# Cross attention: turning the probabilities with transfers of 16-bit halves in place of TensorE transposes

## The chip, the cores and the metric

The kernel runs on one core of a Trainium2 chip. The metric is the device time of one execution in microseconds (us), as the median of several runs. The core has a matrix engine (TensorE, "PE" in the profile; its weight loads are "PEld"), a vector engine (VectorE, "DVE"), a scalar engine (ScalarE, "ACT"), GpSimd ("POOL") and the engine that issues nearly all transfers here (SyncE, "SP"). Each engine runs its own queue of instructions in order and waits on semaphores for the others. SBUF is the on-chip working memory with 128 partitions; PSUM is the small memory that TensorE writes to.

## What is computed

One layer of a perceiver: cross attention of 64 latents per batch to 512 context rows (and to the latents themselves), then self attention over the latents, then a feed-forward part whose weights and activations are quantised to 4 bits. There are 16 batches, 512 channels, and 8 heads of 64 channels in the cross attention, which is all that the change touches:

```python
    def _L0_xattn_ref(x, latents, mask, g_x, b_x, g_l, b_l, w_q, w_kv, w_out, g_o, b_o):
        ...
        xn = _ln(x, g_x, b_x)
        ln = _ln(latents, g_l, b_l)
        q = ln @ w_q
        kv_in = jnp.concatenate([xn, ln], axis=1)
        k, v = jnp.split(kv_in @ w_kv, 2, axis=-1)
        ...
        sim = jnp.einsum('bhid,bhjd->bhij', q, k)
        ...
        attn = jax.nn.softmax(sim, axis=-1)
        out = jnp.einsum('bhij,bhjd->bhid', attn, v)
        out = out.transpose(0, 2, 1, 3).reshape(B, Lq, H * DH)
        return _ln(out @ w_out, g_o, b_o)
```

## The kernel before

**Stages.** First the latents are normalised and projected, and the weights of the keys and values are prepared (`latents`). Then follows the loop over the 16 batches (`cross_attention`), with the quantisation of the feed-forward weights spread over it in small steps (`quant.tick`). Then come the self attention and the feed-forward part. The change lies in the loop over the batches alone.

**One batch.** `keys(b, m)` makes a quarter of the keys, m = 0 to 3: 12 matmuls into one PSUM bank `pk`, which VectorE scales into `k`. `values(b, t)` does the same for a quarter of the values: 12 matmuls into `pv`, which ScalarE scales into `v` (L954). `scores(b, a)` makes the scores of half of the heads (a = 0, 1) into two PSUM tiles `sim`, `softmax(b, a)` has VectorE take the minimum and ScalarE the exponential; the probabilities `pr` come out with the latents on the partitions: 128 partitions (two heads of 64 latents) by 2 (r, two pairs of heads) by 576 columns. The sum of the rows is divided out later. To be the stationary operand of the weighing, the probabilities of the 512 context rows must have the context rows on the partitions. So they are turned.

**The turn.** `turn(b)` turns the probabilities in 32 transposes on TensorE (L1004, 64 x 128 each) into two PSUM tiles `prt`, which come from the same pool of two as the scores (`cm.two`). ScalarE copies these out in four copies (L1013) into `prT`. `turn_latents(b)` turns the last part, the probabilities of the 64 latents, in two transposes (L1023) into `prlt`, which ScalarE copies into `prl`. `finish(b)` then multiplies: `weigh_latents` with `prl` and the latents' values `vl`, then `weigh(b, a, r)` four times with `prT` and `v` into `av`, and `collect` divides by the sums.

**The order.** The loop is written out by hand as a pipeline: in the turn of the loop for batch b, the probabilities of batch b - 1 are turned after the first keys of b, and weighed after the first scores of b. In short, on TensorE:

```python
        keys(b, 0)
        if b:
            turn(b - 1)
            turn_latents(b - 1)
        if done is not None:
            out_turn(done)
        keys(b, 1); keys(b, 2); keys(b, 3)
        scores(b, 0)
        finish(b - 1)
        scores(b, 1)
        values(b, 0); values(b, 1)
        if done is not None:
            out_product(done)
        values(b, 2); values(b, 3)
```

`done` is set in odd batches from 3 on: the output projection of two earlier batches, whose input is turned in `out_turn` (`ot`, 4 transposes) and multiplied in `out_product` (`po`, 12 matmuls). So an odd batch has more work on TensorE than an even one.

**Buffers.** `pk`, `pv`, `ot`, `po` and half of `av` share the three PSUM banks of the pool `mm`: each needs a bank that has been read out. In SBUF, `pr` has two buffers, `prT` four, `v` four; the tag `two_h` (two buffers) holds `prl`, and `two_l` (two buffers) holds `vl`.

**Transfers.** Everything goes through SP's queue, in program order: per batch four loads of the turned context (`raw`, from `fetch`, 256 KB each), one of the context itself (`nat`, 1 MB, from `load`), eight small ones for the latents' keys (`k<-k_d`), four of row factors (`rs_d`), one each of `row`, `mu` and `mask`, two of `vl`, and the loads and stores of the quantised weights (`qw`, `g_d`, `u_d`, `d_d`).

Of the kernel before, what the change touches and what calls it, by code (L numbers as in the profile page):

```python
# [9 lines left out]
F32 = mybir.dt.float32  # L10
F32R = mybir.dt.float32r
U32 = mybir.dt.uint32
U8 = mybir.dt.uint8
AF = mybir.ActivationFunctionType
ALU = mybir.AluOpType
AX = mybir.AxisListType
# [3 lines left out]
P = 128  # L20
D = 512
KC = D // P
B = 16
S = 64
N = 512
NJ = N // P
# [24 lines left out]
class Common:  # L51
# [112 lines left out]
    def shifted(self, dst, src, mv):  # L164

        self.nc.scalar.activation(dst, src, AF.Identity, bias=mv[:, 2:3], scale=mv[:, 1:2])

# [692 lines left out]
def cross_attention(tc, cm, sc, i, cw, cx, w1, w2, att, quant):  # L860

    nc = tc.nc
# [24 lines left out]
    state = {}  # L887
    half = (N + S) // 2

    def begin(b):  # L890
        if b >= B:
            return
        p, e = divmod(b, 2)
        g, n = divmod(b, GB)
        mine = slice(n * S, (n + 1) * S)
        mu = w1.tile([P, N], U8, tag="mu", name=f"mu_{b}")
        nc.sync.dma_start(mu, i["mask"][b : b + 1, :].to_broadcast([P, N]))
        with nc.allow_non_contiguous_dma(reason="the latents of a batch"):
            nc.sync.dma_start(queries[e], sc.q[g][:, :, mine])
        state[b] = dict(mu=mu, k=[], v=[], tot=cm.small.tile([P, KC], F32, tag="tot", name=f"tot_{b}"))  # L900

    def latents_values(b):
        if b >= B:
            return
        p, e = divmod(b, 2)
        vl = state[b]["vl"] = w2.tile([P, KC, S], F32, tag="two_l", bufs=2, name=f"vl_{b}")
        src = sc.v[p][e * S : (e + 1) * S].rearrange("p (n two d) -> p n two d", two=2, d=S)
        for h in range(2):
            nc.sync.dma_start(vl[h * S : (h + 1) * S], src[:, :, h, :])
# [22 lines left out]
    def keys(b, m):  # L932

        k = ends.pop((b, m))
        hi, lo = cx.done[b]
        cols = slice(m * P, (m + 1) * P)
        ps = cm.mm(f"pk_{b}_{m}")
        cm.product(
            ps, lambda c: (w_k[0][:, c, cols], w_k[1][:, c, cols], hi[:, c, :], lo[:, c, :]), range(KC)
        )  # L940
        nc.vector.tensor_tensor(k[:, S : S + N], ps, cx.row[b], ALU.mult)  # L941
        state[b]["k"].append(k)

    def values(b, t):
        hi, lo = cx.done[b]
        cols = slice(t * P, (t + 1) * P)
        ps = cm.mm(f"pv_{b}_{t}")
        cm.product(
            ps,
            lambda k: (hi[:, k, cols], lo[:, k, cols], w_v[0][:, k, :], w_v[1][:, k, :]),  # L950
            range(KC),
        )
        v = w1.tile([P, D], F32, tag="v", bufs=4, name=f"v_{b}_{t}")
        nc.scalar.mul(v, ps, cx.rs[b][:, t : t + 1])  # L954
        state[b]["v"].append(v)
# [18 lines left out]

    def softmax(b, a):
        st = state[b]
        st["pr", a] = w1.tile([P, 2, N + S], F32, tag="pr", bufs=2, name=f"pr_{b}_{a}")

        def two(t):
            return t.rearrange("p (h n) -> p h n", h=2)  # L980

        for r, ps in enumerate(st.pop(("sim", a))):
            mask = masks[b % 2][:, columns_of(r)[0]]
            pr = st["pr", a][:, r, :]
            least = cm.small.tile([P, 1], F32, tag="least", name=f"least_{b}_{a}_{r}")
            nc.vector.tensor_tensor_reduce(  # L986
                two(pr), ps[:, :, :half], two(mask), -1.0, BIG, ALU.add, ALU.min, least
            )
            t = 2 * a + r
            nc.scalar.activation(  # L990
                pr, pr, AF.Exp, bias=least, scale=-1.0, accum_out=st["tot"][:, t : t + 1]
            )

    def turn(b):

        pts = [cm.two(f"prt_{b}_{a}") for a in range(2)]
        for a, pt in enumerate(pts):
            for r in range(2):
                first = columns_of(r)[1].start
                for j in range(NJ):  # L1000
                    at = (r * NJ + j) * S
                    for c in range(2):
                        rows = slice(c * S, (c + 1) * S)
                        nc.tensor.transpose(  # L1004
                            pt[:, c, at : at + S],
                            state[b]["pr", a][rows, r, first + j * P : first + (j + 1) * P],
                            cm.ident[rows, rows],
                        )
        for a, pt in enumerate(pts):
            for r in range(2):  # L1010
                prT = w1.tile([P, NJ, P], F32, tag="prT", bufs=4, name=f"prT_{b}_{a}_{r}")
                src = pt[:, :, r * NJ * S : (r + 1) * NJ * S].rearrange("p c (j q) -> p c j q", q=S)
                nc.scalar.copy(prT.rearrange("p j (c q) -> p c j q", q=S), src)  # L1013
                state[b]["prT", a, r] = prT

    def turn_latents(b):
        st = state[b]
        prl = w2.tile([P, 2, P], F32, tag="two_h", bufs=2, name=f"prl_{b}")
        pt = cm.ps_av.tile([P, D], F32, tag="av", name=f"prlt_{b}")[:, : 2 * P]
        pt = pt.rearrange("p (n q) -> p n q", q=P)  # L1020
        for a in range(2):
            pr = st.pop(("pr", a)).rearrange("p r t -> p (r t)")
            nc.tensor.transpose(pt[:, a, :], pr[:, N : N + P], cm.ident)  # L1023
        nc.scalar.copy(prl, pt)
        st["prl"] = prl

    def weigh_latents(b):

# [123 lines left out]
    for b in range(B):  # L1152

        def tick():
            if b:
                quant.tick()

        done = (b - 3) // 2 if b >= 3 and b % 2 else None
        last = b == B - 1
        keys(b, 0)  # L1160
        if last:
            att.load("Wq")
            att.load("Wk")
        cx.high(b + 1, 0)
        if b >= 4 and b % 2 == 0:
            out_moments((b - 4) // 2)
        if b > 1:
            tick()
        if b:
            turn(b - 1)  # L1170
            turn_latents(b - 1)
        if done is not None:
            out_turn(done)
        keys(b, 1)
        cx.low(b + 1, 0)
        cx.high(b + 1, 1)
        if b > 1:
            tick()
        keys(b, 2)
        if done is not None:  # L1180
            out_low(done)
        cx.fetch(b + 2, 0)
        if b == 0:
            for k in range(KC):
                load_o(k)
        cx.flat(b + 1)
        cx.low(b + 1, 1)
        cx.high(b + 1, 2)
        tick()
        if last:  # L1190
            att.split("Wq", 0, 1)
        if b == 0:
            scores(b, 0)
            softmax(b, 0)
        keys(b, 3)
        cx.fetch(b + 2, 1)
        if b:
            scores(b, 0)
            softmax(b, 0)
        cx.low(b + 1, 2)  # L1200
        cx.high(b + 1, 3)
# [3 lines that stand above are left out]
            softmax(b, 1)  # L1205
            around(b + 1, 2, 3)
            around(b + 2, 0, 1)
        tick()
        values(b, 0)
        cx.every(b + 1)  # L1210
        cx.low(b + 1, 3)
        cx.stats(b + 2, 0)
        tick()
        if last:
            att.split("Wq", 2, 3)
            att.load("Wv")
        if b == 0:
            scores(b, 1)
            softmax(b, 1)
            around(b + 1, 2, 3)  # L1220
            around(b + 2, 0, 1)
        values(b, 1)
        begin(b + 1)
        latents_values(b + 1)
        cx.fetch(b + 2, 2)
        cx.stats(b + 2, 1)
        tick()
        if last:
            att.norm(0)
            att.split("Wk", 0, 1)  # L1230
        tick()
        if done is not None:
            out_product(done)
        tick()
        values(b, 2)
        cx.fetch(b + 2, 3)
        cx.stats(b + 2, 2)
        tick()
        if done is not None:
            out_norm(done)  # L1240
            out_add(done)
        if b == 0:
            weight_o(0)
            weight_o(1)
        if b == 2:
            att.sa.load()
        if b == 5:
            att.sa.work()
        if last:
            att.split("Wk", 2, 3)  # L1250
            att.load("Wo")
            att.turn(0)
        values(b, 3)
        cx.stats(b + 2, 3)
        cx.spread(b + 2)
        mask(b + 1)
        if b == 0:
            weight_o(2)
            weight_o(3)
        quant.tick()  # L1260
        cx.load(b + 3)
    turn(B - 1)
    turn_latents(B - 1)
# [691 lines left out]
```

## Time and profile before

| what | value |
|---|---|
| median of 3 runs | 880.91 us (880.81 to 881.11) |
| the profiled execution | 881.33 us, span 879.5 us |
| TensorE clock granted | 1.0 throughout |
| `prt` on TensorE (L1004), 512 transposes | 19.3 us busy |
| `prlt` on TensorE (L1023), 32 transposes | 7.0 us busy |
| `prT` on ScalarE (L1013), 64 copies | 32.6 us busy, 594 ns each |
| `pr`, the exponential on ScalarE (L990), 64 | 49.1 us busy, 769 ns each |
| `v` on ScalarE (L954), 64 | 43.2 us busy, 684 ns each |
| transfers issued from SP | 109.48 MB, 38.2% of 16 engines' span |

The span is the time from the first to the last instruction in the trace; the execution's own time is a little longer. A line of the groups names the line of code, the engine, the operation, the tile written and the tiles read, the shape, how many there were, their busy time and the mean of one, and then the idle time of the engine ahead of them with what ended it. L121 is the line of a helper that issues nearly all matmuls, so matmuls are told apart by tile. In a timeline each line is a merged run of like instructions with its start and length in us. For SP it shows the issuing of transfers, not their flight.

### The profile page before, as it was taken

The numbers are of one execution on the slowest core, as the hardware profiler recorded it, in microseconds if no ns is written. First come the engines' busy times: TensorE is split into PE (matmuls) and PEld (weight loads), VectorE is DVE, ScalarE is ACT, GpSimd is POOL, SyncE is SP. The second block draws the span as 40 slices with busy tenths as digits, with TensorE's granted clock in tenths as the row PEclk, the third lists the DMA queues.
The fourth block names the chain that finished last, engine by engine and source line by source line (L and its number), as shares of the span: only waits on it lengthen the run. The fifth ranks groups of instructions, "written<-read, shape, count | busy, mean of one in ns | idle before, by whom it ended". The sixth has DMA issues, their size and how long they took to land.

```text
span 879.5 us, 17521 instructions
## 1 busy us (share of the span) xinstructions
PE 871.7 (99%) x6743; PEld 719.2 (82%) x6743; DVE 687.2 (78%) x1457; ACT 398.8 (45%) x787; POOL 296.2 (34%) x341
## 2 busy tenths in 40 slices
PE   8999999999999999999999999999999999999998
PEld 8988787878787888778878888888888888888887
DVE  7734457789788887787888867688998897888876
ACT  5654454544544535354445455554556233332221
POOL 2334234235353352353433622545543120111100
PEclk9999999999999999999999999999999999999999
DMA  8464554644655455435644362240008330000000
GB/s 277 167 233 169 167 163 142 201 143 141 192 164 160 138 174 168 136 111 178 183 134 149 121 198 64 82 192 1 1 3 320 136 144 13 13 13 13 13 12 25
DMA packets 80379, 111.12 MB, mean 126 GB/s; under 512 B 33176, under 2 KB 39080, under 8 KB 79016
## 3 DMA queue, kind: packets, MB, share of 16 engines
q1 hardware_dynamic: 80136, 109.48, 38.2%
q8 instruction: 53, 0.87, 0.4%
q0 software_dynamic: 160, 0.52, 0.2%
q14 instruction: 30, 0.25, 0.1%
HBM read 84.26 MB, written 25.72 MB: 125 GB/s over the span
## 4 chain that ended last, share of the span: by engine, by line
PE 93%; DVE 3%; DMA 2%; ACT 1%; POOL 1%; issue 1%; SPq 0%; ACTq 0%; DVEq 0%; POOLq 0%
PE pv L121 20%; PE pk L121 19%; PE gu L121 13%; PE dn L121 6%; PE sim L967 4%; PE av L1055 4%; PE Wv L121 3%; PE wo L121 3%; PE po L121 2%; PE Wq L121 2%; PE Wk L121 2%; PE prt L1004 2%; PE lq L121 2%; PE lk L121 2%; PE lv L121 1%; PE ht L171 1%
## 5 line engine op out<-in xcount | busy, mean ns | idle before, releaser
L121 PE MATMUL pv<-xvh,x 128*128 128x512 f32 x512 | 133.0, 394 | 0.0
L121 PE MATMUL pk<-x,xkh 128*128 128x512 f32 x512 | 128.2, 392 | 0.0
L121 PEld LDWEIGHTS pv<-xvh,x 128*128 128x128 f32 x512 | 94.8, 188 | 26.2 <-issue 7.0
L121 PEld LDWEIGHTS pk<-x,xkh 128*128 128x128 f32 x512 | 94.9, 188 | 19.5 <-issue 0.4
L990 ACT ACTIVATE pr<-pr,least 128x576 f32<-128x576 f32 x64 | 49.1, 769 | 59.7 <-DVE least L986 59.7
L941 DVE TENSOR_TENSOR k<-pk,row 128x512 f32<-128x512 f32 x64 | 43.2, 675 | 39.2 <-PE pk L121 39.0
L368 POOL TENSOR_TENSOR x<-raw,x 128x512 fp32r<-128x512 f32 x32 | 41.6, 1301 | 85.8 <-ACT x L362 80.5
L121 PE MATMUL pv<-xvl,x 128*128 128x512 f32 x256 | 68.7, 390 | 0.0
L121 PE MATMUL pk<-x,xkl 128*128 128x512 f32 x256 | 68.5, 389 | 0.0
L954 ACT ACTIVATE v<-pv,rs 128x512 f32<-128x512 f32 x64 | 43.2, 684 | 54.8 <-PE pv L121 54.3
L121 PE MATMUL gu<-uT,fx 128*128 128x512 f32 (+1 forms) x288 | 67.0, 377 | 0.2 <-DMA uT<-u_d 0.2
L121 PE MATMUL gu<-gT,fx 128*128 128x512 f32 (+1 forms) x288 | 65.8, 376 | 0.0
L121 PEld LDWEIGHTS gu<-gT,fx 128*128 128x128 f32 x288 | 52.2, 188 | 7.6 <-ACT fx L129 0.2
L121 PEld LDWEIGHTS gu<-uT,fx 128*128 128x128 f32 x288 | 51.8, 188 | 7.7 <-DMA uT<-u_d 0.5
L121 PEld LDWEIGHTS pv<-xvl,x 128*128 128x128 f32 x256 | 48.0, 188 | 10.3
L121 PEld LDWEIGHTS pk<-x,xkl 128*128 128x128 f32 x256 | 48.1, 188 | 10.2
L986 DVE CUSTOM_DVE_ANT_0 pr<-sim,mask 128x576 f32<-128x576 f32 x64 | 45.8, 753 | 5.3 <-PE sim L967 4.3
L205 ACT ACTIVATE qe_h<-qe_h,mmagic 128x512 f32<-128x512 f32 (+1 forms) x24 | 16.5, 687 | 66.7 <-DVE qe_h L202 64.6
L321 DVE BATCH_NORM_STATS2 cst<-nat 128x6 f32<-128x512 f32 x64 | 42.8, 669 | 3.7 <-DMA nat<-in_ctx_dram 3.7
L121 PE MATMUL dn<-dT,hh 128*128 128x512 f32 x170 | 42.9, 392 | 0.0
L967 PE MATMUL sim<-k,mask 64*64 64x288 f32 x512 | 40.4, 415 | 0.3 <-DMA mask<-q_d 0.3
L362 ACT CAST x<-raw 128x512 fp32r<-128x512 f32 x64 | 39.1, 631 | 0.0
(347 smaller groups left out, 1867.1 us busy)
## 6 DMA issues: line engine op xcount, KB each, us to landing
nat<-in_ctx_dram SPq DMA_DIRECT2D x16, 1024.0 KB
raw<-in_ctxT_dram SPq DMA_DIRECT2D x64, 256.0 KB
d_d<-qhl_d SPq DMA_DIRECT2D x11, 512.0 KB
row<-rs_d SPq DMA_DIRECT2D x16, 256.0 KB
g_d<-qhl_g SPq DMA_DIRECT2D x8, 512.0 KB
u_d<-qhl_u SPq DMA_DIRECT2D x8, 512.0 KB
gT<-g_d SPq DMA_DIRECT2D x4, 1024.0 KB
uT<-u_d SPq DMA_DIRECT2D x4, 1024.0 KB
```

The costliest lines, as they stand in the source:

```text
L121: self.nc.tensor.matmul(ps, lhsT=p[i], rhs=p[j], start=start and n == 0, stop=stop and n == last)
L205: nc.scalar.activation(e, e, AF.Relu, bias=self.mmagic, scale=MAGIC)
L321: nc.vector.bn_stats(st, self.nat[b][:, j, :])
L362: self.cm.nc.scalar.copy(self.done[b][0][:, c, :], self.raw[:, c, :])
L368: by.tensor_tensor(lo, self.raw[:, c, :], f32(hi), ALU.subtract)
L941: nc.vector.tensor_tensor(k[:, S : S + N], ps, cx.row[b], ALU.mult)
L954: nc.scalar.mul(v, ps, cx.rs[b][:, t : t + 1])
L967: nc.tensor.matmul(pss[r][c * S : (c + 1) * S, h, :half], lhsT=queries[b % 2][rows, m, :], rhs=st["k"][m][rows, at : at + half], start=Tru ...
L986: nc.vector.tensor_tensor_reduce(two(pr), ps[:, :, :half], two(mask), -1.0, BIG, ALU.add, ALU.min, least)
L990: nc.scalar.activation(pr, pr, AF.Exp, bias=least, scale=-1.0, accum_out=st["tot"][:, t : t + 1])
L1004: nc.tensor.transpose(pt[:, c, at : at + S], state[b]["pr", a][rows, r, first + j * P : first + (j + 1) * P], cm.ident[rows, rows],)
L1055: nc.tensor.matmul(st["av"][r][rows, a, :], lhsT=prT[:, j, rows], rhs=st["v"][j][:, at : at + S], start=False, stop=j == NJ - 1, skip_grou ...
```

## The change

The turn of the context's probabilities leaves TensorE in batches 0 to 14; the last batch keeps `turn`. In its place stand three steps.

`halves(b, a)`: ScalarE takes the 32-bit probabilities of the context columns apart into their lower and upper 16 bits, in two copies of 128 x 1024 16-bit elements (`half`, which takes over the two buffers of `two_h`). `send(b, a)`: SP issues two transposing transfers from SBUF to SBUF, one for each half, 256 KB each, into `far`, which takes a buffer of `pr` (so that pool's buffers now go round as `pr`, `pr`, `far`, `far`; it grows by 64 elements a row to keep the needed columns together). `join(b, a)`: ScalarE writes both halves back into 32-bit `prT`, in two copies (r = 0, 1), each of 1024 16-bit elements, interleaved.

`turn_latents(b)` moves from the next batch's first keys to the place between the second and third values of its own batch, and `prl` becomes the second part of the tile that holds `vl`.

In the order of the program, `halves(b, 0)` stands after the first values, `halves(b, 1)` and then `send(b, 0)` after the third values (the `send` behind the batch's last `raw` load), `send(b, 1)` after the fourth, ahead of the `nat` load; `join(b - 1, 0)` stands after the second keys of the next batch, `join(b - 1, 1)` after the third.

```diff
@@ latents_values
-        vl = state[b]["vl"] = w2.tile([P, KC, S], F32, tag="two_l", bufs=2, name=f"vl_{b}")
+        both = w2.tile([P, 2, KC * S], F32, tag="two_l", bufs=2, name=f"lat_{b}")
+        vl = state[b]["vl"] = both[:, 0].rearrange("p (n d) -> p n d", d=S)
+        state[b]["prl"] = both[:, 1].rearrange("p (n q) -> p n q", q=P)
@@ softmax
-        st["pr", a] = w1.tile([P, 2, N + S], F32, tag="pr", bufs=2, name=f"pr_{b}_{a}")
+        wide = w1.tile([P, 2 * (N + 2 * S)], F32, tag="pr", bufs=2, name=f"pr_{b}_{a}")
+        st["wide", a] = wide.rearrange("p (r n) -> p r n", r=2)
+        st["pr", a] = wide[:, : 2 * (N + S)].rearrange("p (r n) -> p r n", r=2)
@@ new functions
+    def halves(b, a):
+        st = state[b]
+        src = st.pop(("wide", a))[:, :, :N].bitcast(U16).rearrange("p r (n h) -> p h r n", h=2)
+        for h in range(2):
+            half = w2.tile([P, 2, N], U16, tag="two_h", bufs=2, name=f"half_{b}_{a}_{h}")
+            nc.scalar.copy(half, src[:, h])
+            st["half", a, h] = half
+
+    def send(b, a):
+        st = state[b]
+        far = w1.tile([P, 2 * (N + 2 * S)], F32, tag="pr", bufs=2, name=f"far_{b}_{a}")
+        far = far[:, : 2 * N].bitcast(U16).rearrange("p (h n q) -> p h n q", h=2, q=P)
+        for h in range(2):
+            half = st.pop(("half", a, h)).rearrange("p r n -> p (r n)")
+            nc.sync.dma_start(far[:, h], half, transpose=True)
+        st["far", a] = far
+
+    def join(b, a):
+        far = state[b].pop(("far", a))
+        for r in range(2):
+            prT = w1.tile([P, NJ, P], F32, tag="prT", bufs=4, name=f"prT_{b}_{a}_{r}")
+            dst = prT.rearrange("p j q -> p (j q)").bitcast(U16).rearrange("p (n h) -> p n h", h=2)
+            src = far[:, :, r * NJ : (r + 1) * NJ].rearrange("p h j q -> p (j q) h")
+            nc.scalar.copy(dst, src)
+            state[b]["prT", a, r] = prT
@@ turn_latents
-        prl = w2.tile([P, 2, P], F32, tag="two_h", bufs=2, name=f"prl_{b}")
+        prl = st["prl"]
...
-        st["prl"] = prl
@@ the loop over b
         keys(b, 0)
...
-        if b:
-            turn(b - 1)
-            turn_latents(b - 1)
         if done is not None:
             out_turn(done)
         keys(b, 1)
+        if b:
+            join(b - 1, 0)
...
         keys(b, 2)
+        if b:
+            join(b - 1, 1)
...
         values(b, 0)
+        if b and not last:
+            halves(b, 0)
...
         values(b, 1)
+        if b == 0:
+            halves(b, 0)
+        if not last:
+            turn_latents(b)
...
         values(b, 2)
+        if not last:
+            halves(b, 1)
         cx.fetch(b + 2, 3)
+        if not last:
+            send(b, 0)
...
+        if not last:
+            send(b, 1)
         cx.load(b + 3)
```

More of the change, by code (lines that the diff above doesn't have):

```diff
@@ L13 @@
 U8 = mybir.dt.uint8
+U16 = mybir.dt.uint16
 AF = mybir.ActivationFunctionType
```

## The prediction

> **What bounds the kernel now.** I read the page first, then one pair of batches in order of time on TensorE, ScalarE and the queue of SP. From the page: the span, the engines, the chain, and the group of instructions that the change removes.
>
> ```profile
> span 879.5 us, 17521 instructions
> ...
> PE 871.7 (99%) x6743; PEld 719.2 (82%) x6743; DVE 687.2 (78%) x1457; ACT 398.8 (45%) x787; POOL 296.2 (34%) x341
> ...
> PE 93%; DVE 3%; DMA 2%; ACT 1%; POOL 1%; issue 1%; SPq 0%; ACTq 0%; DVEq 0%; POOLq 0%
> ```
>
> TensorE works 99% of the span and carries 93% of the chain, so a TensorE instruction taken out is worth its whole time, as long as nothing else falls late. The table of stretches for batch 8 alone (columns: stretch, length, then PE, PEld, DVE, ACT, POOL, clock, DMA share, GB/s) says what room the others have:
>
> ```profile
> 314.41:342.51 28.10, 28.10 (x244) 22.51 (x243) 23.40 (x53) 13.65 (x28) 13.01 (x15) 1.00 0.48 144
> ```
>
> PE has none; ScalarE works 13.65 of 28.10 us; the transfers fill 0.48. The timeline of TensorE at the seam of batches 8 and 9 (start, length, engine, line, what):
>
> ```profile
> 341.60 1.07 PE L121 MATMUL pv<-xvh,x 128*128 128x512 f32 x4
> 342.51 1.98 PE L121 MATMUL pk<-x,xkh 128*128 128x512 f32 x8
> 344.32 1.07 PE L121 MATMUL pk<-x,xkl 128*128 128x512 f32 x4
> 345.32 1.21 PE L1004 MATMUL prt<-ident,pr 64*128 64x64 f32 x32
> 346.46 0.44 PE L1023 MATMUL prlt<-ident,pr 128*128 128x128 f32 x2
> 346.73 0.60 PE L171 MATMUL ot<-ident,o 128*128 128x128 f32 x4
> 347.09 1.17 PE L121 MATMUL pk<-x,xkh 128*128 128x512 f32 x4
> ```
>
> The 32 turns of `prt` hold TensorE from 345.32 to 346.46, 1.14 us; in batch 8 (317.23 to 318.37) again 1.14. An odd batch has `ot` between its first and second keys, which an even batch has not. SP's queue just before:
>
> ```profile
> 334.01 0.58 SPq L281 DMA_DIRECT2D qw_g<-in_w_gate_dram  x1
> ...
> 339.40 0.68 SPq L281 DMA_DIRECT2D qw_g<-in_w_gate_dram  x1
> 340.19 0.37 SPq L354 DMA_DIRECT2D raw<-in_ctxT_dram  x1
> ```
>
> SP issues almost without a gap from 328.21 (`k<-k_d`, released by the scores) to 340.56, some 0.58 us each; then it is nearly idle until 344.16. That hole is where the first new transfers land.
>
> **The change, part by part.**
>
> *TensorE.* 32 turns leave each of 15 batches (the last keeps them): 15 x 1.14 = 17.1 us. The two `prlt` turns only move behind the second values; cost nothing. Below zero the saving could reach further only through the scores' PSUM tiles, which `prt` shared: their second group took 1.59 instead of 1.20 us in one of two batches seen, so at most 0.4 x 15 = 6 us more. I take 17.1.
>
> *ScalarE.* Out go 4 `prT` copies (L1013, 594 ns); in come 4 `half` copies and 4 joins of 1024 elements. The trace has no 16-bit copy; the nearest row is 1024 wide:
>
> ```profile
> L1456 ACT ACTIVATE ex<-ex 128x1024 f32<-128x1024 f32 x8 | 8.5, 1062 | 22.6 <-DVE ex L1447 22.6
> ```
>
> 8 x 1.06 - 4 x 0.59 = +6.1 us, so 13.65 becomes 19.8 us of a 27.0 us batch. By the sum it is hidden under TensorE. By 512-element rows a copy could not be cheaper than 0.59; at twice 1.06 (a penalty for strided 16-bit access) ScalarE would hold 28.3 us: rival C.
>
> *The moved step and its queue.* SP gets four transposing transfers of 256 KB per batch: two after the last `raw` load of the batch, two more behind the next weight load or store. What they pass is `nat`, used a batch later, and the next batch's `raw`, `rs_d` and `k` loads, which have SP's gaps (10 us in batch 8) as cover. The wait that matters is on ScalarE. `half` has two buffers, so the second pair of `half` copies must wait until the first two transfers of the batch have landed, and they stand ahead of the fourth `v` copy. Behind that copy is PSUM: the `mm` pool has three banks, and as built, the second keys of an odd batch (after `ot`, which takes one bank) wait for it; in an even batch, without `ot`, only the third keys do.
>
> Call T the time from SP's start on the first transfer to the landing of the second. Seam 8/9, an even batch: without `prt` the next keys start at 342.51 - 1.14 = 341.37, take 2.81, `ot` 0.36, so the second keys are due at 344.54. Before them must fit a `half` copy (1.06) and the `v` copy (L954, 0.69): the landing is due at 342.79. SP comes free at 340.19 + 0.37, shifted with TensorE by 1.14: 339.42. Slack: 3.4 us. Seam 7/8, an odd batch: third keys at 321.41, less 2.28 for two batches' turns, 319.13, less 1.75 = 317.38; SP is free at 309.57 + 0.55 - 1.14 = 308.98. Slack: 8.4 us. So, with 7 tight seams (batches 2, 4 to 14) and 8 loose ones:
>
> change = -17.1 + 7 x max(0, T - 3.4) + 8 x max(0, T - 8.4).
>
> It turns from gain to loss at T = 3.4 + 17.1 / 7 = 5.8 us.
>
> *T itself.* No transposing transfer is in the trace. Landing: the `qw_g` load issued at 334.01 released VectorE at 336.69 (it had idled 0.20 us for it), 2.68 us after the start of the issue, 2.10 after its end. Issue, low end: one plain issue, 0.58, so T = 2 x 0.58 + 2.1 = 3.3, no stall, -17.1. High end: such a transfer turns eight squares of 128 x 128, and each costs a plain issue: 4.64, T = 11.4, stalls 7 x 8.0 + 8 x 3.0 = 80, +63. Between them I take the nearest row that issues one turned thing in pieces, the four small `rs_d` issues:
>
> ```profile
> 326.14 1.28 SPq L342 DMA_DIRECT2D rs_d<-rsT  x4
> ```
>
> 0.32 each, eight squares 2.56. T = 5.1 + 2.1 = 7.2; 7 x 3.8 = 26.6 us of stalls in the even batches, none in the odd ones. The second pair then needs 2 x 2.56 + 2.1 after its last `half` and lands before the joins are due.
>
> A page bears on T and stands against my value. The Trainium skill, "Advanced Engine Details and Errata", section "X-Bar Transpose (TRN2)", has transposing transfers as fast as plain ones at 350 to 400 GB/s; by it the sum is the low end, about 864 us. The same skill, "VectorE: DVE Perf Modes", section "The three transpose paths", gives 1309 ns for one 128 x 128 square of 16 bits by transfer against 390 ns on TensorE; if the eight squares of a transfer ran one after another, an estimate from that page is 10.5 us a transfer and well over 1000 us in all. No run here shows either yet.
>
> *Sum.* The profiled execution took 881.3 us (span 879.5, 1.8 around it). 881.3 - 17.1 + 26.6 = 890.8; it stands 0.4 above the median of the runs, which leaves the forecast at 891.
>
> **Rivals.**
>
> A, faster: the transfers behave like plain ones. For it: ScalarE, SP and the transfers all have room by their sums, and a plain load lands in 2.7 us. Against: the slack in even batches is only 3.4 us, and the `v` copies there already came late (both at 342.25, behind a quantiser step). 881.3 - 17.1 = 864. It decides as long as T stays under 5.8.
>
> B, much slower: the transfers move in small pieces and fill the queues. Eight `k` loads in 256-byte rows together with one 256 KB `raw` took 1.24 us of DMA time (shares 0.49, 0.53 and 0.22 in the stretches 328 to 331); the `raw` alone takes 0.70 at the 377 GB/s of the stretch from 321; that leaves 0.54 for 512 rows on 16 engines, 17 ns a row. Written in 32-byte pieces a transfer is 8192 / 16 x 17 ns = 8.7 us, T = 0.58 + 17.4 + 2.1 = 20, and 7 x 16.6 + 8 x 11.6 - 17 = +192: 1073 us. At half of that, 4.35 us a transfer, T is 11.4 again, 944 us, and the four transfers (17.4) with the 13.5 already there overfill a 27 us batch: from there on it decides.
>
> C: ScalarE's strided 16-bit copies cost 2.12 us. Each even seam is late by 1.06 more, and ScalarE's 28.3 us exceed 27.0 there by 1.3: 891 + 7 x 2.4 = 908.
>
> **How the numbers follow.** Forecast 0.40 (T from 4.5 to 10: 872 to 924), A 0.33, B 0.22, C 0.05. The forecast's 891 is the likeliest. The range reaches down past A by part of the 6 us above, 860, and up into B as far as T = 14 (74 + 45 - 17 = +102), 985; some 0.15 of B lies beyond, with a little of the others 0.2. A difference of 0.2% is about what these measurements tell from none. Faster: A and the forecast's lower edge, 0.35; same 0.04; slower 0.61.
>
> **What would show it.** Right: TensorE idle of some 4 us before the second keys of odd batches (`pk`, after `ot`), none of it before `av`; on ScalarE the second `half` pair idle for the DMA; each transposing issue 2 to 3 us on SP. A shows as issues near 0.6 us and a gapless TensorE at 864. B shows as a DMA share near 1 in the cross attention and joins waiting for `far`, with idle before `av` in every batch. C shows as `half` copies near 2 us. It is wrong if T is under 5.8, or if TensorE waits elsewhere, first of all for the joins.

## The result and the profile after

The changed kernel takes 907.26 us as the median of 4 runs (906.33 to 908.31), against 880.86 (879.66 to 881.11) for the kernel before in the same session: ratio 1.0303, interval 1.0285 to 1.0321. It is slower by 26 us where 10 were forecast.

The page of the changed kernel (span; busy time of the engines; the row of the clock, in tenths; the queue of SP with packets, MB and share; the chain; the two new groups on ScalarE):

```profile
span 905.9 us, 16783 instructions
...
PE 868.8 (96%) x6263; PEld 712.6 (79%) x6263; DVE 685.0 (76%) x1457; ACT 488.6 (54%) x847; POOL 298.6 (33%) x341
...
PEclk9999989999998999999999999999999999999999
...
q1 hardware_dynamic: 143496, 125.22, 47.8%
...
PE 65%; DMA 14%; DVE 9%; ACT 6%; SPq 3%; issue 2%; POOL 1%; DVEq 0%; ACTq 0%; POOLq 0%
...
L1027 ACT COPY half<-pr 128x1024 uint16<-128x1024 uint16 x60 | 59.8, 1042 | 43.8 <-DMA far<-half 43.8
...
L1047 ACT COPY prT<-far 128x1024 uint16<-128x1024 uint16 x60 | 67.2, 1171 | 0.0
```

480 transposes are gone from TensorE (6743 instructions became 6263), yet it is busy only 2.9 us less, and its share of the chain fell from 93% to 65%. Transfers now carry 14% of the chain, half of it `far<-half`. The `half` copies stood idle for 43.8 us behind those transfers. The joins waited for nothing.

TensorE's own waits (line waited for; us in all, times, longest), where the kernel before had nothing longer than 0.3 us in the loop over the batches:

```profile
PE pk L122 <- ACT v L957: 12.4, 7, 3.0
PE sim L970 <- DVE least L991: 9.3, 6, 1.9
PE av L1088 <- ACT prT L1047: 4.4, 2, 2.8
PE prlt L1057 <- ACT pr L995: 1.6, 1, 1.6
...
PE av L1072 <- ACT v L957: 0.8, 1, 0.8
```

These are three different things. The first line is the seam that the prediction spoke of. One of the seven, at batches 8 and 9, over all engines:

```profile
360.45 3.80 SPq L1037 DMA_TRANSPOSE far<-half  x2
...
365.00 1.99 ACT L1027 COPY half<-pr 128x1024 uint16<-128x1024 uint16 x2 [1.94 <-DMA far<-half]
...
365.82 0.60 PE L172 MATMUL ot<-ident,o 128*128 128x128 f32 x4
...
366.90 0.68 ACT L957 ACTIVATE v<-pv,rs 128x512 f32<-128x512 f32 x1
...
367.63 2.09 PE L122 MATMUL pk<-x,xkh 128*128 128x512 f32 x8 [1.21 <-ACT v L957]
```

The landing at 365.00 releases two `half` copies; only then comes the `v` copy that frees a PSUM bank, and the second keys behind `ot` start 1.21 us late.

The second line, the scores waiting for VectorE's minimum, is new and was not forecast. The chain of waits (start, length, what) leads there from a late transfer in an odd batch:

```profile
329.08 6.41 DMA far<-half
...
337.56 0.53 ACT qhl_u L289
...
340.93 7.08 DMA u_d<-qhl_u
...
348.10 0.10 DVE qhl_g L288
...
348.60 0.65 DVE k L944
349.25 0.67 DVE pr L991
...
349.99 1.44 PE sim L970 x12
```

While ScalarE stands behind `half`, the quantiser's cast (L289) stands behind ScalarE. Its store goes out late, after the 1 MB `nat` load, and lands 7.08 us later; VectorE waits for it with `k` and the minimum queued behind. TensorE's scores then stood 1.63 us. The other three lines are the first batches, which are special (batch 1 has no earlier work to hide the joins of batch 0).

The rest of the loss goes with the clock. The profile by stretches of 1 us around one of the longest seams (columns: stretch, length, then PE, PEld, DVE, ACT, POOL, clock, DMA share, GB/s) and TensorE there:

```profile
242.00:243.00 1.00, 0.89 (x4) 0.77 (x5) 0.71 (x1) 1.00 (x3) 1.00 (x2) 1.00 0.29 58
243.00:244.00 1.00, 1.00 (x5) 0.77 (x4) 0.00 (x0) 1.00 (x4) 0.08 (x1) 0.58 1.10 211
244.00:245.00 1.00, 1.00 (x4) 0.81 (x3) 0.00 (x0) 1.00 (x4) 0.00 (x0) 0.50 2.32 55
```

```profile
242.11 2.89 PE L122 MATMUL pk<-x,xkh 128*128 128x512 f32 x8 [2.84 <-ACT v L957]
244.80 1.91 PE L122 MATMUL pk<-x,xkl 128*128 128x512 f32 x4
246.51 2.04 PE L122 MATMUL pk<-x,xkh 128*128 128x512 f32 x8
```

After standing 2.84 us TensorE runs about 3.4 us at half clock: four matmuls take 1.91 us, elsewhere 1.07. Summed over stretches of 1 us, the clock's shortfall in the loop is 12.0 us, in five dips (127 to 134, 243 to 247, 287 to 295, 427 to 431 and 492 to 496), each beside a wait of the list; 11.0 us of it fell on busy TensorE. In the loop of the kernel before there is none. (A further dip, from 7.6 to 11.1, lies ahead of the loop.)

So the span's 26.4 us divide as follows. TensorE's idle time rose from 7.8 to 37.1 us: 12.4 at the seams, 9.3 at the scores, 6.8 in the first batches, 0.8 ahead of the loop. Its busy time fell by 2.9: with the 11.0 us of dips taken out, by 13.9.

### The profile page after: what moved, and what is told of

Its sections match the earlier page's. It is cut to its first block, busy times and chain, and to the rows that moved or that the text cites. A ratio compares the mean times of both kernels' runs of the same rounds, so it can differ in the third digit from the quotient of the medians.

```text
span 905.9 us, 16783 instructions
## 1 busy us (share of the span) xinstructions
PE 868.8 (96%) x6263; PEld 712.6 (79%) x6263; DVE 685.0 (76%) x1457; ACT 488.6 (54%) x847; POOL 298.6 (33%) x341
## 3 DMA queue, kind: packets, MB, share of 16 engines
q1 hardware_dynamic: 143496, 125.22, 47.8%
## 4 chain that ended last, share of the span: by engine, by line
PE 65%; DMA 14%; DVE 9%; ACT 6%; SPq 3%; issue 2%; POOL 1%; DVEq 0%; ACTq 0%; POOLq 0%
PE gu L122 13%; PE pk L122 10%; DMA far<-half 7%; PE dn L122 6%; PE pv L122 6%; PE sim L970 4%; ACT half L1027 3%; PE Wv L122 2%; PE wo L122 2%; PE av L1088 2%; PE lv L122 2%; DMA g_d<-qhl_g 2%; PE Wq L122 2%; PE Wk L122 2%; DMA u_d<-qhl_u 2%
## 5 line engine op out<-in xcount | busy, mean ns | idle before, releaser
L122 PE MATMUL pk<-x,xkh 128*128 128x512 f32 x512 | 130.7, 398 | 12.4 <-ACT v L957 12.4
L122 PE MATMUL pv<-xvh,x 128*128 128x512 f32 x512 | 136.6, 399 | 0.0
L122 PEld LDWEIGHTS pk<-x,xkh 128*128 128x128 f32 x512 | 97.7, 192 | 34.9 <-ACT v L957 14.1
L122 PEld LDWEIGHTS pv<-xvh,x 128*128 128x128 f32 x512 | 95.2, 190 | 26.6 <-issue 7.6
L1027 ACT COPY half<-pr 128x1024 uint16<-128x1024 uint16 x60 | 59.8, 1042 | 43.8 <-DMA far<-half 43.8
L1047 ACT COPY prT<-far 128x1024 uint16<-128x1024 uint16 x60 | 67.2, 1171 | 0.0
L970 PE MATMUL sim<-k,mask 64*64 64x288 f32 x512 | 44.8, 430 | 9.6 <-DVE least L991 9.3
```

Of the source, the lines that this page charges most:

```text
L122: self.nc.tensor.matmul(ps, lhsT=p[i], rhs=p[j], start=start and n == 0, stop=stop and n == last)
L970: nc.tensor.matmul(pss[r][c * S : (c + 1) * S, h, :half], lhsT=queries[b % 2][rows, m, :], rhs=st["k"][m][rows, at : at + half], start=Tru ...
L1027: nc.scalar.copy(half, src[:, h])
L1047: nc.scalar.copy(dst, src)
```

## The experiments

Three groups: what is in the loss (e1 to e4, e12 and e14), whether the second pair's place or the first pair's time mends it (e5 to e7), and what the scores need (e8 to e11, e13). All ratios are to the kernel before on the same chip.

| kernel | median us | ratio, interval | TensorE waits in the loop, us |
|---|---|---|---|
| changed | 907.26 | 1.0303 [1.0285, 1.0321] | seam 12.4, scores 9.3, joins 4.4 |
| e1 plain copies | 899.95 | 1.0221 [1.0192, 1.0251] | seam 13.5, scores 3.1, joins 4.5 |
| e2 no transfers | 877.53 | 0.9975 [0.9943, 1.0006] | seam 6.2, scores 1.7 |
| e3 four `half` buffers | 879.55 | 0.9982 [0.9965, 1.0000] | seam 5.9, scores 3.0 |
| e4 transfers beside | 940.97 | 1.0687 [1.0654, 1.0721] | seam 6.7, scores 28.2 |
| e5 halves early | 881.87 | 1.0021 [1.0011, 1.0031] | scores 4.8, joins 3.6 |
| e6 sent early | 902.08 | 1.0249 [1.0223, 1.0276] | seam 7.3, scores 5.9, joins 4.5, keys for `oz` 3.7 |
| e7 both early | 894.33 | 1.0161 [1.0141, 1.0182] | scores 9.3, joins 5.0 |
| e8 two stores | 879.45 | 0.9989 [0.9978, 0.9999] | scores 4.0, joins 4.3 |
| e9 e8, steps moved, batch 0 | 874.89 | 0.9940 [0.9926, 0.9955] | keys for `k` 6.6, seam 2.3 |
| e10 changed, steps moved | 912.32 | 1.0365 [1.0347, 1.0382] | seam 18.6, joins 4.7, `ot` for `v` 3.8 |
| e11 before, steps moved | 889.17 | 1.0102 [1.0084, 1.0119] | seam 4.4, keys for `k` 1.6 |
| e12 before, no turns | 869.65 | 0.9873 [0.9858, 0.9887] | scores 4.8 |
| e13 e8, batch 0 | 873.40 | 0.9908 [0.9891, 0.9925] | scores 2.5, joins 2.0, keys for `oz` 2.1 |
| e14 changed, batch 0 | 899.61 | 1.0213 [1.0194, 1.0233] | seam 13.0, scores 9.5 |

"Seam" is the keys waiting for a `v` copy, "scores" is `sim` waiting for VectorE's minimum, "joins" is `av` waiting for `prT`. Only the largest waits of each run are listed.

**e1: does the turning cost anything?** The same transfers without transposition; the probabilities arrive unturned.

```diff
-            nc.sync.dma_start(far[:, h], half, transpose=True)
+            nc.sync.dma_start(far[:, h].rearrange("p n q -> p (n q)"), half)
```

> The four transfers of a batch copy the halves as they are, without turning them (the output is not the reference's). Theory (the landing of the first pair holds ScalarE at the seam): a plain issue is 0.58 us, so the second of a pair lands 3.3 us after the start of the first, under the slack of 3.4; the second keys of odd batches stop waiting for the v copy (12.4 us in the changed kernel, near 0 here), and the clock dips that follow these waits go too: 868 to 880 us. Rival (any 256 KB of extra traffic in that place does it): the wait stays above 8 us and the time above 895. Rival (ScalarE's own added work): the same, above 895.

899.95: plain copies cost nearly as much. The groups of e1 on ScalarE:

```profile
L1027 ACT COPY half<-pr 128x1024 uint16<-128x1024 uint16 x60 | 59.7, 1042 | 36.0 <-DMA far<-half 36.0
```

From the first issue to the release of `half` a plain pair took 4.6 us as the median, a transposing pair 4.9. Issuing is what differs: 0.59 us against 1.33 a transfer. The seam is as late as in the changed kernel (13.5); the 7.3 us between the two kernels are found at the scores, 3.1 instead of 9.3, in agreement with a shorter hold on SP's queue ahead of the quantiser's stores.

**e2: no transfers at all.** The joins read the unturned probabilities; the `half` copies stay.

```diff
-            half = st.pop(("half", a, h)).rearrange("p r n -> p (r n)")
-            nc.sync.dma_start(far[:, h], half, transpose=True)
+            st.pop(("half", a, h))
```

> No transfers at all: ScalarE does all its 16-bit copies, the joins read the unturned probabilities (the output is not the reference's). Theory (waits for transfers are the whole loss): TensorE runs without gaps in the batches and keeps its 17 us: 863 to 868 us, clock 1.0. Rival (ScalarE's added 6.7 us a batch are what is late): above 885 us, TensorE still waits for v copies or exponentials.

877.53, some 10 us above what was expected. Four seams are still late (6.2 us in all, at most 1.8), with no transfer to wait for: two `half` copies of 1.04 us stand between the third and fourth `v` copies.

**e3: four buffers for `half`.** The halves take turns in the four buffers of `prT`, so no `half` copy waits for a transfer. All else, the transposing transfers included, is as in the change.

```diff
-            half = w2.tile([P, 2, N], U16, tag="two_h", bufs=2, name=f"half_{b}_{a}_{h}")
+            half = w1.tile([P, 2, N], U16, tag="prT", bufs=4, name=f"half_{b}_{a}_{h}")
```

> The halves get four buffers, those of prT, so that ScalarE never waits for a landing before the second pair; nothing else changes, transfers and their turning stay. Theory: the waits of half for far (43.8 us on ScalarE) and of the second keys for v (12.4 us on TensorE) go, with three of the clock dips behind them (some 5 us): 885 to 892 us; the waits of the scores for VectorE (9.3 us) and those of the first batch (5.2 us) stay, if they have a cause of their own. Rival (the blocked ScalarE also delays the quantiser and so VectorE): the scores' waits go as well, 872 to 882 us. Rival (the wait only moves on to the joins): above 900 us, idle before av.

The rival is met: 879.55. The waits of e3:

```profile
PE pk L122 <- ACT v L957: 5.9, 5, 1.8
PE sim L970 <- DVE least L991: 3.0, 3, 1.9
PE prlt L1057 <- ACT pr L995: 2.8, 1, 2.8
```

Both the seam and the scores fell, although e3 moves the same bytes in the same packets (143496). So the wait at the scores came mainly from the blocked ScalarE and not from the traffic alone. This one edit gives back 27.7 us, more than the whole loss.

**e4: traffic without the rest.** The kernel before, with four transposing transfers a batch into a spare tile that nothing reads.

```diff
+        for h in range(2):
+            nc.sync.dma_start(
+                side.rearrange("p (n q) -> p n q", q=P), rows_o["g_o"].bitcast(U16), transpose=True
+            )
```

> The kernel before, with four transposing transfers of 256 KB a batch put into SP's queue at the places of the change, from a constant tile into a spare one that nobody reads; each waits for the one before it. Theory (only the wait of ScalarE for them costs): 880 to 884 us, TensorE without gaps. Rival (their traffic or their place in SP's queue delays the quantiser's stores, and so VectorE and the scores): the scores wait for VectorE 5 us or more, 888 us or more.

940.97, far beyond either. All four write one tile, so each waits for the one before and SP stands for it (a pair held it 7.36 us at 344.43). The waits of VectorE in e4 show what that does:

```profile
DVE qhl_g L288 <- DMA g_d<-qhl_g: 19.0, 6, 6.4
DVE qhl_u L288 <- DMA u_d<-qhl_u: 19.0, 7, 4.4
```

This is not the load of the changed kernel, so its price can't be carried over; it does show the path from a held SP queue over the quantiser's stores to VectorE and the scores (28.2 us).

**e12: what were the turns worth?** The kernel before without `prt`; `prT` is copied from the unturned probabilities.

```diff
-        pts = [cm.two(f"prt_{b}_{a}") for a in range(2)]
-        for a, pt in enumerate(pts):
...
+                src = state[b]["pr", a][:, r, columns_of(r)[1]]
+                nc.scalar.copy(prT.rearrange("p j q -> p (j q)"), src)
```

> The kernel before without its turns of the context's probabilities, in all batches, and with nothing in their place; the four copies of a batch read the unturned probabilities from SBUF (the output is not the reference's). It measures what the removal alone is worth. If a TensorE instruction is worth its whole time there: 16 x 1.14 = 18 us, 862 to 864 us, no gaps. If VectorE, with at most 0.9 us to spare at the scores, takes over: the scores wait in many batches, 867 to 874 us.

869.65: 11 us for 16 batches, not 18. TensorE's busy time falls from 871.7 to 856.8, which is 14.9 us, 0.93 a batch; the changed kernel's, less its dips, fell by 13.9 for 15 batches. The 14.9 is already a balance: 19.3 us of `prt` went, and the matmuls of the scores, held apart inside their groups, take up 44.3 us in place of 40.4. Of the 14.9, a third comes back as waits:

```profile
PE sim L967 <- DVE least L986: 4.8, 6, 0.9
```

This is not spread evenly. The starts of scores in the kernel before, for batches 4, 5, 8, 9 and 10 (the first scores of each):

```profile
207.36 1.20 PE L967 MATMUL sim<-k,mask 64*64 64x288 f32 x16
...
235.85 1.20 PE L967 MATMUL sim<-k,mask 64*64 64x288 f32 x16
...
326.94 1.20 PE L967 MATMUL sim<-k,mask 64*64 64x288 f32 x16
...
355.44 1.20 PE L967 MATMUL sim<-k,mask 64*64 64x288 f32 x16
...
386.25 1.20 PE L967 MATMUL sim<-k,mask 64*64 64x288 f32 x16
```

And in e12, with the second scores of batch 4, which wait and take longer:

```profile
204.52 1.20 PE L967 MATMUL sim<-k,mask 64*64 64x288 f32 x16
...
208.52 1.86 PE L967 MATMUL sim<-k,mask 64*64 64x288 f32 x16 [0.55 <-DVE least L986]
...
233.05 1.20 PE L967 MATMUL sim<-k,mask 64*64 64x288 f32 x16
...
324.25 1.20 PE L967 MATMUL sim<-k,mask 64*64 64x288 f32 x16
...
351.50 1.20 PE L967 MATMUL sim<-k,mask 64*64 64x288 f32 x16
...
381.00 1.20 PE L967 MATMUL sim<-k,mask 64*64 64x288 f32 x16
```

From one batch's first scores to the next's, batches 8 and 9, where nothing waits, are 1.25 and 1.31 us shorter (28.50 to 27.25, 30.81 to 29.50). Batch 4 is not shorter at all (28.49 to 28.53). In the kernel before, the turns between the keys had given VectorE the time to be ready for the scores.

**e5: the second pair of `half` ahead of the third `v` copy** (from e3; batch 0's latents are turned later).

```diff
+        elif not last:
+            halves(b, 1)
...
         values(b, 2)
-        if not last:
+        if b == 0:
             halves(b, 1)
+            turn_latents(b)
```

> As the run with four half buffers, and the second pair of half copies stands ahead of the third v copy (after the second values, in batch 0 after the third), so that no 16-bit copy stands between a batch's last two v copies; batch 0 turns its latents after the third values. Theory (what was left, 5.9 us at the second keys and 2.8 us in batch 0, is the place of the half copies in ScalarE's queue, and the clock dips follow from the gaps): both go, with most of the clock loss (0.992 there): 866 to 872 us, correct. Rival (ScalarE is too full, wherever the copies stand): the waits move to the scores or to the first v copies, 877 us or more.

881.87. The seam is gone, as meant, but the scores wait 4.8 us in 8 places and the time is no better than that of e3.

**e6 and e7: the first pair sent two loads earlier**, in the changed kernel (e6) and in e5 (e7).

```diff
+        if b and not last:
+            send(b, 0)
...
-        if not last:
+        if b == 0:
             send(b, 0)
```

> The changed kernel with its two half buffers, only the first pair of transfers goes into SP's queue two loads earlier (behind the third raw load and the latents' tables, in place of behind the fourth raw load). Theory (the landing of the first pair holds ScalarE, and what counts is when it is issued and what is ahead of it): it is issued some 2 us earlier, the waits of half for far fall from 43.8 to some 20 us, those of the second keys from 12.4 to about 6 us: 888 to 896 us. Rival (the transfers' own length, not their place, decides): above 902 us.

> Half copies early with four buffers, and the first pair of transfers early as well. Theory: no wait depends on the landing any more, so the place of the transfers changes little against the half copies alone: 865 to 872 us. Rival (the transfers' traffic delays the quantiser's stores): the scores' wait for VectorE grows, 875 us or more.

e6 did what its theory said to the waits (`half` 43.8 to 15.4, seam 12.4 to 7.3) and gained only 5 us. e7 lost 12 us against e5: scores 9.3. The transfers now stand ahead of the quantiser's loads and stores in SP's queue, and those reach VectorE late.

**e8: the quantiser's pieces in two buffers.** From e5; the two freed `two_h` buffers hold every other piece, with two stores for it.

```diff
+        self.turns = getattr(self, "turns", 0) + 1
+        if self.turns % 2:
+            hl = self.w1.tile([P, 2, D], F32R, tag="q_hl", name=f"qhl_{name}")[:, :, :n]
...
+            hi, lo = (
+                self.w2.tile([P, D], F32R, tag="two_h", bufs=2, name=f"qhl_{name}_{h}")[:, :n] for h in range(2)
+            )
```

> Half copies early with four buffers, and every other piece of the quantiser puts its two parts into the two buffers that the halves have left, with two stores, so that VectorE need not wait for the store of the piece before. Theory (the scores' waits for VectorE come from the quantiser's turn, which waits for a store that the new transfers delay): the 3.0 us left of them go: 1 to 4 us less than without it, 863 to 870 us. Rival (VectorE is late because ScalarE hands it its inputs late): no difference beyond 1 us.

879.45, 2.4 us less than e5, the waits at the scores 4.8 to 4.0.

**e9, e10, e11: two steps of the quantiser moved** from the keys to the values, so that VectorE has less to do before the scores: in e8 with batch 0 kept on TensorE (e9), in the changed kernel (e10), and in the kernel before, as a control (e11).

```diff
-        if b > 1:
-            tick()
         keys(b, 2)
...
-        tick()
...
         cx.stats(b + 2, 0)
         tick()
+        if b > 1:
+            tick()
...
         cx.stats(b + 2, 2)
+        tick()
         tick()
```

> The run with two stores, and two quantiser steps a batch moved from the keys to the values, so that VectorE has less ahead of the scores' minimum; batch 0 keeps its turn on TensorE (there the joins came late: 4.3 us and a clock dip in batch 1). Theory (with the turns gone from between the keys, the scores come 1.1 us earlier and VectorE, which had at most 0.9 us to spare there, is late): the scores' waits (4.0 us, and 0.66 us within each of these groups) and batch 1's go: 864 to 870 us, correct. Rival (VectorE's place is not it; ScalarE hands over late): the waits stay, 875 us or more.

> The changed kernel with nothing altered but the two quantiser steps a batch moved from the keys to the values. Theory: the scores' waits for VectorE (9.3 us, some 4 us more within the groups, and one clock dip of 3 us) go, the waits at the second keys (12.4 us) stay: 889 to 897 us. Rival (the landing alone holds everything): within 3 us of the changed kernel's 907.

> The control: the kernel before with the two quantiser steps moved in the same way. TensorE had no gaps there, so nothing to gain by any theory: 879 to 882 us.

The scores wait in none of the three, yet e10 and e11 are slower than what they were made from, by 5 and 9 us. The waits of the control, e11, show where:

```profile
PE pk L121 <- ACT v L954: 4.4, 5, 1.2
PE pk L121 <- DVE k L941: 1.6, 3, 0.6
```

The moved steps now stand ahead of the `v` copies on ScalarE and of `k` on VectorE: the lateness has moved from the scores to the keys. e9 was faster than both kernels, with two edits in it; the next two runs part them.

**e14 and e13: batch 0 kept on TensorE**, as in the kernel before, in the changed kernel (e14) and in e8 (e13).

```diff
+        if b == 1:
+            turn(0)
+            turn_latents(0)
...
         keys(b, 1)
-        if b:
+        if b > 1:
             join(b - 1, 0)
...
-        if not last:
+        if b and not last:
             send(b, 0)
```

> The changed kernel with batch 0 kept as in the kernel before: its probabilities are turned on TensorE after the first keys of batch 1, no halves, transfers or joins for it; all else as changed. In the changed kernel's trace TensorE waited in batch 1 1.6 us for the latents' turn, 0.8 for the values' copy and 4.4 us for the joins, and the clock dipped behind them. Theory that these 6.8 us are lost time of their own: less 6.8, plus 1.1 for the turns, 907.3 becomes 900 to 902. Rival: batch 1's stall only stood where later work caught up (the quantiser ran on in it), so the time stays within 905 to 909.

> e8_two_stores with batch 0 on TensorE as before, and the quantiser's steps left where they were (e9_less_before_scores had both edits and took 874.9). Theory: batch 1's waits for the joins (4.3 us) go, 1.1 us of turns come: 879.5 becomes 875 to 877 and the moved steps gave e9_less_before_scores next to nothing. By the control e11_before_ticks, where moving the steps alone cost 8.7 us, leaving them could even give 868 to 872. Rival: the moved steps were what gave the 4.6 us, since they take load from VectorE ahead of the scores; then this kernel stays at 878 to 880, with about 4 us of waits at the scores.

e14 took 899.61, 7.7 us less than the changed kernel: batch 1's waits were lost time of their own. e13 took 873.40, the fastest version found that computes everything: 0.9908 [0.9891, 0.9925], without the moved steps, so these gave e9 nothing. TensorE in e13 waits almost nowhere:

```profile
PE sim L981 <- DVE least L1002: 2.5, 3, 1.4
PE pk L122 <- DVE oz L156: 2.1, 1, 2.1
PE av L1099 <- ACT prT L1058: 2.0, 1, 2.0
```

It is 7.5 us faster than the kernel before and, by the medians, 3.7 us slower than e12 (on another chip), which pays nothing for the turning; e13 keeps two of the 16 turns on TensorE.

## Why the prediction was half right

**The place and mechanism of the seam: right.** Idle TensorE was forecast before the second keys of odd batches, behind `ot`, from a `v` copy behind a `half` pair waiting for its transfer. Seven such waits are there, and e3 removes more than half of their time by taking the `half` wait away.

**Their size: half.** 26.6 us were forecast, 12.4 measured. T was taken as 7.2 from an issue of 2.56; the issue took 1.33, longest 3.27, so eight small issues were the wrong row. But the landing did not shrink with it. The first of a pair landed 4.9 us after SP's start (4.2 to 6.5), plain copies in 4.6: the prediction's 2.1 behind the issue, taken from one `qw_g` load of 192 KB, was too little. It had also read SP's idle time as a hole for the transfers. That SP issues nothing does not mean that nothing is in flight; the stretches of the kernel before, in that hole, have a DMA share (last but one) of 0.82 to 0.95:

```profile
340.00:341.00 1.00, 1.00 (x6) 0.83 (x5) 0.38 (x2) 0.51 (x1) 0.00 (x0) 1.00 0.82 195
341.00:342.00 1.00, 1.00 (x6) 0.84 (x5) 1.00 (x3) 0.27 (x1) 0.00 (x0) 1.00 0.95 325
```

While the `qw_g` load was under way (334 to 337) it was 0.15, 0.66 and 0.97, and while the first transfer of seam 8/9 was (360 to 365) 1.03 to 1.28. That the full engines set the landing fits this, but no run varied them alone.

Since the two `half` copies follow each other without a pause, the second transfer lands at most one copy later, and T is about 4.9 + 1.06 = 6.0 at most. That gives up to 7 x 2.6 = 18 us of stalls. The loose seams did not stall, as forecast, but their lateness reached the scores through VectorE.

**The removal: the price right, its worth too large.** 17.1 was 15 x 1.14, the time from first to last record of the turns. In e12 a batch in which nothing waits is 1.25 to 1.31 us shorter, so the price was not too high. But in others nothing is gained, and all 16 together give 11 us. The page's 99% hid that VectorE was within a microsecond of the scores:

```profile
DVE pr L986 <- PE sim L967: 4.3, 10, 0.9
```

This line of the kernel before says that VectorE waited for the scores 10 times and never longer than 0.9. The prediction asked only who fills the hole on ScalarE and SP. A reader of that view could have seen that the next to be late, with TensorE 1.14 us a batch shorter, is VectorE.

**"None of it before `av`": wrong for batch 1.** The sum was made for a steady batch and multiplied. Batch 0 has its `halves` later and nothing to hide them, and cost 7.7 us (e14).

**The step that failed is the sum itself**: -17.1 plus the seams. With T as measured it would be at most -17.1 + 18 = +1, no change. What made it +26 are terms that it did not have or had at nothing: a blocked ScalarE delays the quantiser's casts, its stores and so VectorE's minimum (9.3 us at the scores, 3.0 in e3); batch 1 (7.7); and the low clock beside five of the waits, 11.0 us of busy TensorE.

Run against run the loss divides so: without the turns 11 us less (e12), with the `half` copies and the new joins in their place 8 more (e2 against e12), with the transfers 30 more (the changed kernel against e2). The prediction's terms for these were -17.1, 0 and +26.6. That the last is near is luck: its seams were twice those measured, and the rest came from the terms that it lacked. The 0 stood for ScalarE's copies because their sum fits under TensorE; in e2 the sum fits too, and four seams are late. (e2 also moves the latents' turn and keeps the last batch's, so the 8 us are not the copies' alone.)

**The rivals.** A, transfers like plain ones, is half true and useless: they land like plain ones, and plain ones cost 899.95 in e1, not 864. B's small pieces are there in part (143496 packets in place of 80136, 1056 more a transfer, where B counted 8192), but e3 moves them at 879.55. C is out: the strided 16-bit copies took 1042 and 1171 ns, not 2120.

**The two pages.** By the Trainium skill, "Advanced Engine Details and Errata", section "X-Bar Transpose (TRN2)", transposing transfers are as fast as plain ones. The landing nearly agrees (4.9 us against 4.6), the issue doesn't (1.33 against 0.59). The estimate of 10.5 us a transfer from the table of "VectorE: DVE Perf Modes" is ruled out: the first transfer of a pair had landed within 6.5 us in every batch, so its squares do not run one after another at that price.

**Still open.** How the 9.3 us at the scores divide between ScalarE's wait and SP's hold was seen only by e1 and e3 together, which each take some of both. Why a transfer of 256 KB needs 4.6 to 4.9 us in the loop is open too. That a dip of the clock comes from the wait before it is read from their order in the traces; no run changed the one without the other.

## What to carry to other kernels

Before moving work off a full engine, ask of each other engine how early it is at the next point where the full one needs it, and price what lies behind every new wait in the order of its queue: here one two-buffer tile ahead of a PSUM copy was worth 28 us. A copy that waits for a transfer belongs behind whatever else its engine owes to others, or needs enough buffers never to wait. First and last iterations get a sum of their own. And a gap in the queue that issues transfers is no gap in flight: read the DMA share there.

## What the runs showed of the hardware

The TensorE clock fell to 0.50 behind waits that were shorter than expected: after 1.90, 2.21, 2.84 and 2.96 us of idle TensorE in the changed kernel's loop, and not after 2.15, 1.89 or 1.74 in the same run. A dip lasted about 3.4 us or twice that: behind the 1.90 us at 286.95 the clock's shortfall from 287 to 295 sums to 3.4 us, which is 6.8 us at half clock. The Trainium skill, "TensorE: Matmul & The Clock Gate", section "Part 1: The HAM clock gate (the 'warmup' mystery)", puts the fall behind at least one idle window of some 3.4 us, and has that window run freely. The lengths of the dips agree with such a window; the idle times don't, since none of these reached 3.4 us, and the measurement decides.

The starts agree with it as well. By the trace's clock records the five dips begin at 127.11, 243.16, 287.53, 427.48 and 492.33 (the 0.58 of the stretch 243 to 244 gives 243.16 too). These lie 34, 13, 41 and 19 times 3.413 us apart, and in every run with more than one dip the starts lie whole multiples of that apart. Cut by this grid, the windows just ahead of the five dips held 1.90 to 2.83 us of idle TensorE, and no other window of the loop at full clock more than 1.64. The wait of 2.15 us that brought no dip (177.59 to 179.75) lies across two windows, with 0.71 and 1.44 us in each. How much idle time it takes is not settled: in other runs a window with 1.16 us had a dip behind it (e8) and one with 1.92 us had none (e7).

A plain copy of 256 KB from SBUF to SBUF released its waiter only after 4.6 us in the loop (median), though its issue took 0.59; a transposing one took 4.9, so the turning adds little to it.
